# An LSTM step on one core: the cell update as a scan, with its gates' activations and a register load in other places

## The chip, the core and the metric

The program runs on one core of one Trainium2 chip, in a single launch. The metric is the device time of one execution in microseconds; several executions are summarised by their median. A core has engines that run side by side, each with its own in-order stream of instructions: TensorE (PE, with its weight loads shown as PEld), VectorE (DVE), ScalarE (ACT), GpSimd (POOL) and SyncE (SP, which issues DMAs). They meet through semaphores. An engine's sequencer reads its instructions and does the control work itself (register loads, branches, semaphore instructions); in the profile its records have the engine's name with a q behind it.

## The reference

Eight stages follow one another on a matrix x of 625 nodes by 512 features: four graph stages and four feed-forward ones. The change lies in the sixth, an LSTM over the 625 rows with four sets of weights. At each step the state chooses the set:

```python
def _lstm_activate(gates, c):
    i, f, g, o = jnp.split(gates, 4, axis=-1)
    c_new = jax.nn.sigmoid(f) * c + jax.nn.sigmoid(i) * jnp.tanh(g)
    h_new = jax.nn.sigmoid(o) * jnp.tanh(c_new)
    return (h_new, c_new)
...
def step(carry, x_t):
    h, c = carry
    sel_in = jnp.concatenate([h, c, x_t], axis=-1)
    logits = sel_in @ W_sel.T + b_sel
    onehot = jax.nn.one_hot(jnp.argmax(logits, axis=-1), Sx, dtype=x_t.dtype)
    g_all = jnp.einsum('bi,sgi->bsg', x_t, W_ih) + jnp.einsum('bh,sgh->bsg', h, W_hh) + b_ih + b_hh
    g = jnp.einsum('bsg,bs->bg', g_all, onehot)
    h2, c2 = _lstm_activate(g, c)
    return ((h2, c2), h2)
...
x = x + _L2_ffn_ref(_layernorm(x, axis=-1)[None], L2_ffn_W_ih, L2_ffn_W_hh, L2_ffn_b_ih, L2_ffn_b_hh, L2_ffn_W_sel, L2_ffn_b_sel)[0]
```

The batch is 1, H is 512, so each step is a product of one vector of 512 with a 512 by 2048 matrix, chosen by an argmax over four logits, and then some arithmetic on 512 numbers.

## The kernel before

`L2_ffn` prepares the stage. It multiplies all inputs with the input weights ahead of time into `gx`, splits the recurrent weights of the gates i, f and g into three bfloat16 parts (`wp`, L1591 to L1600) and keeps those of o in float32 (`wo`). The order of gates is i, f, g, o (`g` = 0, 1, 2, 3 in the code). Weights and inputs of g (`g == 2`) are multiplied by 2 at L1596, L1770 and L1772. It also computes, for each row and each of the four sets, a base for guessing the next step's set (`xv`, L1696 to L1733) from what the input alone says of the gates.

`recurrence` (L1820) is written by hand, outside the scheduler: one program for each engine, with semaphores set and waited for by name (`sem["c"]`, `sem["th"]` and so on). A vector of 512 lies as 128 partitions by 4 columns. The 625 steps run as 125 blocks of 5; inputs of a block are fetched by SyncE three blocks deep. One step goes like this:

- VectorE makes the new hidden state hT as `th` times `so` (L2092) and splits it into three bfloat16 parts (L2094, L2096).
- TensorE computes the logits in `lg`: the part of the cell state first (L1972, which waits for `c`), then the input row (L1974), then the part of hT (L1977). It doesn't wait for their argmax: it branches by a guess, made one step earlier, to the code of one of the four sets, runs a quarter of the output gate's matmuls (L2013) and 40 of the 48 matmuls of i and f into `pa` (L2016). Only then does it load the true choice into a register (L2018). If the guess was right, it goes on in the body `rest`; if not, it branches to `missed` and does those matmuls again with the right set.
- In `rest` follow the last 8 matmuls into `pa`, 48 for g into `pb` (twelve times four, L2025 to L2026), the output gate's other three quarters into `po` (L2028, L2030, both through L1993), one float32 matmul of a product needed much later (L2032, into `later`), and then the load of the next guess into a register (L2033, L2034) and the branch to the next step.
- VectorE meanwhile finds the argmax of the logits (`ix`) and the next guess (`gi`, L2107), turns `pa` (L2115), sums its parts into the first eight columns of `ga` (L2117: i and f), does the same with `pb` (L2119, L2121: g), and turns `po` (L2123).
- ScalarE takes tanh of half of all 12 columns of `ga` in one instruction (L2062, into `act4`), since sigmoid(v) is half of 1 + tanh(v/2). VectorE makes `prod` (L2126), which holds (1 + tanh(i/2)) tanh(g) and (1 + tanh(f/2)) times the kept state, and from it the new state (L2131), which is kept doubled as `c2`. Between the two it adds up the output gate (`go`, L2129). ScalarE takes sigmoid of `go` (L2064, `so`), then tanh of half of `c2` (L2066, `th`), and the step closes.

GpSimd does nothing in the loop but clear semaphores, in two ranges, `late` (after the logits) and `early` (after the first part of `ga`, L1958 to L1960, which then raises `ce`). VectorE waits for `ce` at L2124.

## Time and profile before

| what | value |
|---|---|
| time, median of 3 runs | 4764.43 us (4754.03 to 4769.32) |
| profiled execution | 4754.91 us, span 4753.1 us |
| mean granted TensorE clock | 0.965 |
| first and last L2092 in the recurrence's loop | 1519.9 and 4392.3 us |
| TensorE busy in the span | 4370.0 us (92%) |
| VectorE busy in the span | 2715.8 us (57%) |
| ScalarE busy in the span | 1231.4 us (26%) |

The profile is of one execution; its span runs from the first to the last instruction. Section 2 of its page cuts this span into 40 slices of 119 us, where a digit is a busy share in tenths:

```profile
PE   8998997799998999999999999999999999999888
...
DVE  7535015521264666666666666666666666666258
ACT  8533111211163222222222222222111111111136
```

The even stretch from the 13th slice to the 37th is the recurrence. Section 5 lists the costliest groups of instructions (line, engine, operation, tiles and shapes, count; then busy time, mean ns of one; then the engine's idle time before them and what ended it):

```profile
L1984 PE MATMUL pa<-wp,left 128*23 128x256 bf16 x32080 | 1003.3, 273 | 0.0
...
L1984 PE MATMUL pb<-wp,left 128*23 128x128 bf16 x30000 | 531.5, 219 | 0.0
...
L2064 ACT ACTIVATE so<-go 128x4 f32<-128x4 f32 x625 | 128.2, 205 | 282.5 <-DVE go L2129 282.5
```

Matmuls are pipelined: each of `pb`'s takes 219 ns, but they overlap. 30000 is 625 times 48.

### The profile page before, as it was taken

The numbers are of one execution on the slowest core, as the hardware profiler recorded it, in microseconds if no ns is written. First come the engines' busy times: TensorE is split into PE (matmuls) and PEld (weight loads), VectorE is DVE, ScalarE is ACT, GpSimd is POOL, SyncE is SP. The second block draws the span as 40 slices with busy tenths as digits, with TensorE's granted clock in tenths as the row PEclk, the third lists the DMA queues.
The fourth block names the chain that finished last, engine by engine and source line by source line (L and its number), as shares of the span: only waits on it lengthen the run. The fifth ranks groups of instructions, "written<-read, shape, count | busy, mean of one in ns | idle before, by whom it ended". The sixth has DMA issues, their size and how long they took to land. (4 is left out here: it accounts for less than half of the span.)

```text
span 4753.1 us, 246181 instructions
## 1 busy us (share of the span) xinstructions
PE 4370.0 (92%) x103068; PEld 3316.7 (70%) x103068; DVE 2715.8 (57%) x14167; ACT 1231.4 (26%) x4816; POOL 148.5 (3%) x152
## 2 busy tenths in 40 slices
PE   8998997799998999999999999999999999999888
PEld 6666764466566777777777777777777777777555
DVE  7535015521264666666666666666666666666258
ACT  8533111211163222222222222222111111111136
POOL 0000002300000000000000000000000000000011
PEclk9997997899999999999999999999999999999888
DMA  1131973611165122222222222221000000000200
GB/s 42 42 137 57 325 247 118 226 59 56 56 223 161 39 45 42 44 46 42 46 43 45 45 44 46 45 42 34 7 8 7 7 7 9 7 7 4 83 14 12
DMA packets 484662, 305.37 MB, mean 64 GB/s; under 512 B 287068, under 2 KB 385752, under 8 KB 483822
## 3 DMA queue, kind: packets, MB, share of 16 engines
q1 hardware_dynamic: 466554, 279.16, 21.6%
q0 software_dynamic: 8800, 16.92, 1.3%
q10 hardware_dynamic: 9092, 6.87, 0.6%
q8 instruction: 81, 1.33, 0.1%
q14 instruction: 135, 1.10, 0.1%
HBM read 256.29 MB, written 46.54 MB: 64 GB/s over the span
## 5 line engine op out<-in xcount | busy, mean ns | idle before, releaser
L1984 PE MATMUL pa<-wp,left 128*23 128x256 bf16 x32080 | 1003.3, 273 | 0.0
L1984 PEld LDWEIGHTS pa<-wp,left 128*23 128x23 bf16 x32080 | 800.1, 93 | 86.8 <-issue 0.3
L1993 PE MATMUL po<-w,left 128*1 128x128 f32 x15080 | 590.3, 273 | 4.9 <-issue 4.0
L1984 PE MATMUL pb<-wp,left 128*23 128x128 bf16 x30000 | 531.5, 219 | 0.0
L2062 ACT ACTIVATE act<-ga 128x12 f32<-128x12 f32 x625 | 132.7, 212 | 1481.2 <-DVE ga L2121 1481.2
L1984 PEld LDWEIGHTS pb<-wp,left 128*23 128x23 bf16 x30000 | 484.0, 94 | 4.6
L2115 DVE STREAM_TRANSPOSE col<-pa 128x256 f32<-128x256 f32 x625 | 281.7, 451 | 331.7 <-PE pa L1984 331.2
L1972 PE MATMUL pb<-wsel,act 128*4 128x8 f32 x5000 | 217.5, 170 | 178.3 <-DVE act L2131 162.1
L1972 PEld LDWEIGHTS pb<-wsel,act 128*4 128x4 f32 x5000 | 150.1, 83 | 329.3 <-DVE act L2131 312.4
L1993 PEld LDWEIGHTS po<-w,left 128*1 128x1 f32 x15080 | 314.9, 83 | 32.7 <-issue 15.6
L2032 PE MATMUL acc<-xslot,wslot 128*128 128x160 f32 x1250 | 336.9, 351 | 0.0
L2032 PEld LDWEIGHTS acc<-xslot,wslot 128*128 128x128 f32 x1250 | 185.8, 188 | 140.2 <-issue 140.2
L2057 ACT COPY xrow<-xlb 1x4 f32<-1x4 f32 x625 | 122.4, 196 | 538.4 <-ACTq L2055 538.4
L2123 DVE STREAM_TRANSPOSE col<-po 128x128 f32<-128x128 f32 x625 | 198.3, 317 | 92.9 <-PE po L1993 34.3
L2111 DVE COPY col<-gxb 128x16 f32 x625 | 114.1, 183 | 215.5 <-issue 215.5
L1977 PE MATMUL pb<-wsel,left 128*4 128x8 f32 x5000 | 217.5, 170 | 4.0 <-DVE left L2092 2.4
L1993 PE MATMUL po<-wo,left 128*1 128x128 f32 x5336 | 209.6, 272 | 4.7 <-issue 4.7
L2092 DVE TENSOR_TENSOR left<-th,so 128x4 f32<-128x4 f32 x625 | 104.3, 167 | 188.8 <-ACT th L2066 188.7
L2064 ACT ACTIVATE so<-go 128x4 f32<-128x4 f32 x625 | 128.2, 205 | 282.5 <-DVE go L2129 282.5
L2119 DVE STREAM_TRANSPOSE col<-pb 128x128 f32<-128x128 f32 x625 | 191.8, 307 | 1.0 <-PE pb L1984 1.0
L1977 PEld LDWEIGHTS pb<-wsel,left 128*4 128x4 f32 x5000 | 150.1, 83 | 60.1 <-DVE left L2092 6.0
L562 PE MATMUL wide<-hot_dst,hot_src 125*125 125x512 bf16 x640 | 178.0, 391 | 12.6 <-DVE hot_dst L542 12.6
(551 smaller groups left out, 6577.0 us busy)
## 6 DMA issues: line engine op xcount, KB each, us to landing
ring<-in_L_ffn_W_dram SPq DMA_DIRECT2D x80, 1024.0 KB
xslot<-xTd SPq DMA_DIRECT2D x384, 80.0 KB
wslot<-in_L_ffn_WihT_dram SPq DMA_DIRECT2D x384, 64.0 KB
gxb<-gx SPq DMA_DIRECT2D x124, 160.0 KB
w<-in_L_ffn_WihT_dram SPq DMA_DIRECT2D x16, 1024.0 KB
raw<-in_L_ffn_WhhT_dram SPq DMA_DIRECT2D x24, 512.0 KB
made<-ys SPq DMA_DIRECT2D x39, 256.0 KB
w<-in_L_gnn_Wl_dram SPq DMA_DIRECT2D x8, 1024.0 KB
```

Source lines behind the costliest of these rows:

```text
L562: nc.tensor.matmul(wide[i], hs[:, k], hd[:, :W0], start=first, stop=last)
L1972: pe.matmul(lg, c2[:, s:s + 1].to_broadcast([128, S]), wsel[:, 1, s], start=s == 0, stop=False)
L1977: m = pe.matmul(lg, hT[:, s:s + 1].to_broadcast([128, S]), wsel[:, 0, s], start=False, stop=s == KC - 1)
L1984: m = pe.matmul(out[32 * j:32 * j + 2 * GAP + 1], upper[:, s], wp[e][:, s, i, j, gs[0]:gs[1]].rearrange("p g n -> p (g n)"), start=k == 0, ...
L1993: m = pe.matmul(po[32 * j:32 * j + 1].rearrange("p (u r) -> p u r", r=32), left[:, s, 0:1], wo[e][:, s].rearrange("p (u j r) -> p j u r", ...
L2032: pe.matmul(later, wslot, xslot, start=False, stop=True, skip_group_check=True).then_inc(used)
L2057: act.copy(xrow[:, :S], xlb[b % DEEP][:, :, u + 1]).then_inc(sem["x"])
L2062: act.activation(act4[:, 0:3].rearrange("p g s -> p (g s)"), ga, AF.Tanh, scale=0.5).then_inc(sem["ifg"])
L2064: act.activation(so, go, AF.Sigmoid).then_inc(sem["so"])
L2115: dve.transpose(col[:, :8, :32], pa.rearrange("p (b r) -> p b r", r=32)).then_inc(sem["ta"])
L2119: dve.transpose(col[:, 8:12, :32], pb.rearrange("p (b r) -> p b r", r=32)).then_inc(sem["tb"])
L2123: dve.transpose(col[:, 12:, :32], po.rearrange("p (s r) -> p s r", r=32)).then_inc(sem["to"])
```

## The change

The state is kept as it is and not doubled, so the halving of the selection weights for it (L1630) goes. The tiles are new: `seq` is three rows of eight columns, `cs` eight columns whose odd ones (`cell_c`) are the state.

ScalarE now takes sigmoid of i and f (`ga[:, :8]`) as soon as the first part of `ga` is there, into the odd columns of two rows of `seq`, and raises the new semaphore `if`. tanh of g, into the even columns of the third row, follows when the second part is there. Then come tanh of the state and after it sigmoid of the output gate, in the opposite order to before. The new call for g has no scale, and the doubling at L1596, L1770 and L1772 stays.

VectorE multiplies sigmoid of f with the old state into the odd columns of the third row of `seq`, ahead of turning `po`. The wait for `ce` comes ahead of that turn too. One `tensor_tensor_scan` over eight columns then makes the new state: it walks along the columns with a running value, which it multiplies with a column of the first row and to which it adds a column of the third. The even columns of the first row are zero, so an even column gives tanh(g), and the odd one behind it sigmoid(i) tanh(g) + sigmoid(f) c. The sum for the output gate comes after the scan. hT now waits for `th` and for `so`.

TensorE loads the next guess amid the matmuls of g, after the sixth of their twelve groups of four, and no longer at the end of `rest`.

```diff
-            nc.vector.tensor_scalar_mul(wsel[:, 1], wsel[:, 1], 0.5)
...
-    act4, so = t_([128, 4, 4], "act4"), t_([128, 4], "so")
-    c2 = act4[:, 3]
-    prod = t_([128, 2, 4], "prod")
+    seq, cs, so = t_([128, 3, 8], "seq"), t_([128, 8], "cs"), t_([128, 4], "so")
+    cell_c = cs[:, 1::2]
...
-    nc.vector.memset(act4, 0.0)
+    nc.vector.memset(seq, 0.0)
...
-    late = "g x a ta b tb ga ifg o to ao pr c so th".split()
+    late = "g x a ta b tb ga if ifg o to ao pr c so th".split()
...
-                        pe.matmul(lg, c2[:, s:s + 1].to_broadcast([128, S]), wsel[:, 1, s], start=s == 0, stop=False)
+                        pe.matmul(lg, cs[:, 2 * s + 1:2 * s + 2].to_broadcast([128, S]), wsel[:, 1, s], start=s == 0, stop=False)
...
                         for k in range(12):
                             ms = list(gates(e, pb, (2, 3), k))
+                            if k == 5:
+                                pe.wait_ge(sem["g"], 1)
+                                pe.reg_load(guess, gi[e:e + 1, 0:1])
                         ms[-1].then_inc(sem["b"])
...
-                        pe.wait_ge(sem["g"], 1)
-                        pe.reg_load(guess, gi[e:e + 1, 0:1])
                         pe.br(name("next"))
...
+                    act.wait_ge(sem["ga"], 1)
+                    act.activation(seq[:, 0:2, 1::2], ga[:, :8].rearrange("p (g s) -> p g s", g=2), AF.Sigmoid).then_inc(sem["if"])
                     act.wait_ge(sem["ga"], 2)
-                    act.activation(act4[:, 0:3].rearrange("p g s -> p (g s)"), ga, AF.Tanh, scale=0.5).then_inc(sem["ifg"])
+                    act.activation(seq[:, 2, 0::2], ga[:, 8:], AF.Tanh).then_inc(sem["ifg"])
+                    act.wait_ge(sem["c"], 1)
+                    act.activation(th, cell_c, AF.Tanh).then_inc(sem["th"])
                     act.wait_ge(sem["ao"], 1)
                     act.activation(so, go, AF.Sigmoid).then_inc(sem["so"])
-                    act.wait_ge(sem["c"], 1)
-                    act.activation(th, c2, AF.Tanh, scale=0.5).then_inc(sem["th"])
...
                         wait("th")
+                        wait("so")
                         dve.tensor_tensor(hT, th, so, ALU.mult).then_inc(sem["h"])
...
+                        wait("if")
+                        dve.tensor_tensor(seq[:, 2, 1::2], seq[:, 1, 1::2], cell_c, ALU.mult).then_inc(sem["pr"])
+                        wait("ce").then_inc(sem["ce"], -1)
                         wait("o")
                         dve.transpose(col[:, 12:, :32], po.rearrange("p (s r) -> p s r", r=32)).then_inc(sem["to"])
-                        wait("ce").then_inc(sem["ce"], -1)
+                        wait("pr")
                         wait("ifg")
-                        dve.scalar_tensor_tensor(prod, act4[:, 0:2], 1.0, act4[:, 2:4], op0=ALU.add, op1=ALU.mult
-                                                 ).then_inc(sem["pr"])
+                        dve.tensor_tensor_scan(cs, seq[:, 0], seq[:, 2], 0.0, op0=ALU.mult, op1=ALU.add).then_inc(sem["c"])
                         wait("to")
                         dve.tensor_tensor(go, col[:, 12:, 0], col[:, 12:, 3 * GAP], ALU.add).then_inc(sem["ao"])
-                        wait("pr")
-                        dve.scalar_tensor_tensor(c2, prod[:, 1], 0.5, prod[:, 0], op0=ALU.mult, op1=ALU.add
-                                                 ).then_inc(sem["c"])
```

More of the change, by code (lines that the diff above doesn't have):

```diff
@@ L2060, in _ @@
                         m.then_inc(free[b % DEEP][1])
+                    act.wait_ge(sem["ga"], 1)
+                    act.activation(seq[:, 0:2, 1::2], ga[:, :8].rearrange("p (g s) -> p g s", g=2), AF.Sigmoid).then_inc(sem["if"])
                     act.wait_ge(sem["ga"], 2)
-                    act.activation(act4[:, 0:3].rearrange("p g s -> p (g s)"), ga, AF.Tanh, scale=0.5).then_inc(sem["ifg"])
+                    act.activation(seq[:, 2, 0::2], ga[:, 8:], AF.Tanh, scale=0.5).then_inc(sem["ifg"])
+                    act.wait_ge(sem["c"], 1)
+                    act.activation(th, cell_c, AF.Tanh).then_inc(sem["th"])
                     act.wait_ge(sem["ao"], 1)
                     act.activation(so, go, AF.Sigmoid).then_inc(sem["so"])
-                    act.wait_ge(sem["c"], 1)
-                    act.activation(th, c2, AF.Tanh, scale=0.5).then_inc(sem["th"])
                     if n < len(LATER) and n % 4 == 3:
@@ L2082, in _ @@
                 dve.tensor_copy(xrow[:, :S], xlb[0][:, :, 0]).then_inc(sem["x"])
-                dve.memset(c2, 0.0).then_inc(sem["c"])
+                dve.memset(cs, 0.0).then_inc(sem["c"])
+                dve.memset(th, 0.0).then_inc(sem["th"])
+                wait("th")
                 dve.memset(so, 0.0).then_inc(sem["so"])
-                wait("so")
-                dve.memset(th, 0.0).then_inc(sem["th"])
                 for b in range(BLOCKS):
@@ L2135, in _ @@
                 wait("th")
+                wait("so")
                 dve.tensor_tensor(hist[:, N], th, so, ALU.mult)
```

## The prediction

> **What bounds the kernel now.** I read the page's busy row first, then busy time in three stretches, then who waited for whom, then one step of the recurrence in order of time, and last the records of TensorE's own queue (its sequencer), which the order of time leaves out.

> The recurrence runs from 1519.9 to 4396.6 us: 2876.7 of the span's 4753.1 us, in 625 steps that each begin with L2092. The 624 distances between them average 4.603 us. TensorE is busy in 2692 of those 2877 us, but the steps are serial: what counts is the chain inside one step. This one, from the middle, took 4.45 us from hT to hT (2401.76 to 2406.21); its second half:

> ```profile
> 2403.75 0.85 PE L1984 MATMUL pb<-wp,left 128*23 128x128 bf16 x48
> 2404.06 0.45 DVE L2115 STREAM_TRANSPOSE col<-pa 128x256 f32<-128x256 f32 x1 [0.41 <-PE pa L1984]
> 2404.37 0.60 PEld L1993 LDWEIGHTS po<-w,left 128*1 128x1 f32 x24
> 2404.42 0.84 PE L1993 MATMUL po<-w,left 128*1 128x128 f32 x24
> 2404.54 0.20 DVE L2117 TENSOR_REDUCE ga<-col 128x8 f32<-128x32 f32 x1
> 2404.66 0.30 DVE L2119 STREAM_TRANSPOSE col<-pb 128x128 f32<-128x128 f32 x1
> 2405.00 0.18 DVE L2121 TENSOR_REDUCE ga<-col 128x4 f32<-128x16 f32 x1
> ...
> 2405.21 0.21 ACT L2062 ACTIVATE act<-ga 128x12 f32<-128x12 f32 x1 [2.24 <-DVE ga L2121]
> 2405.33 0.32 DVE L2123 STREAM_TRANSPOSE col<-po 128x128 f32<-128x128 f32 x1 [0.15 <-PE po L1993]
> 2405.57 0.12 DVE L2126 SCALAR_TENSOR_TENSOR prod<-act 128x8 f32<-128x8 f32 x1
> 2405.68 0.17 DVE L2129 TENSOR_TENSOR go<-col 128x4 f32<-128x4 f32 x1
> ...
> 2405.76 0.16 DVE L2131 SCALAR_TENSOR_TENSOR act<-prod 128x4 f32<-128x4 f32 x1
> 2405.88 0.20 ACT L2064 ACTIVATE so<-go 128x4 f32<-128x4 f32 x1 [0.46 <-DVE go L2129]
> ...
> 2405.99 0.19 ACT L2066 ACTIVATE th<-act 128x4 f32<-128x4 f32 x1
> ...
> 2406.21 0.17 DVE L2092 TENSOR_TENSOR left<-th,so 128x4 f32<-128x4 f32 x1 [0.29 <-ACT th L2066]
> ```

> Columns: start, duration, engine, line, operation, and the idle time before it with what ended it. The tail to see: TensorE's output-gate matmuls end at 2405.26, VectorE turns them at 2405.33, and only after this (back to back, 0.24 us later) come prod, go and c2; ScalarE then does sigmoid of go, and tanh of c2 behind it. hT waits for that tanh, L2066. An engine's answer starts some 0.03 us after the result it waits for.

> ```profile
> ACT act L2062 <- DVE ga L2121: 1481.2, 625, 4.3
> ...
> DVE left L2092 <- ACT th L2066: 188.7, 624, 0.8
> ```

> This, from the waits (total, times, longest), shows that hT waits for th in every step, and that ScalarE idles over 2 us per step before L2062: room for another activation.

> ```profile
> L2018 PEldq TENSOR_LOAD <-ix x677: 298/302/417, 1522.2 to 4393.3; - x170
> L2034 PEldq TENSOR_LOAD <-gi x625: 298/302/315, 1525.4 to 4395.0; - x157
> ```

> A register load holds TensorE's sequencer for 0.302 us. L2018 ran 677 times in 625 steps: 52 guesses missed, each with the 40 matmuls again. Steps with a hit have a median of 4.447 us, missed ones 6.105: a miss costs 1.658.

> **The change, part by part**, on the step above, +/- where another step differs.

> Scan for prod and c2. f times c (128x4; by go's row 0.165) needs sigmoid of f only. ga's first eight columns are ready at 2404.74, so that sigmoid runs 2404.77 to 2404.98 (L2062's 0.21) in ScalarE's idle time; f times c goes behind L2121 at about 2405.10, in VectorE's 0.15 idle before L2123. Cost nothing; without that cover it would cost the 0.085 to 0.12 that separates such instructions' starts. tanh of g stays where L2062 was. The scan takes prod's place at 2405.57. The trace of before has no scan: nearest rows are prod's 0.124 (same 128x8) and the 0.203 of L2117 (128x32). I take 0.165, the usual small VectorE operation. The state is ready at 2405.735 instead of 2405.92.

> Tanh before sigmoid. th runs from 2405.77; go keeps its place (it needs the transpose's end, 2405.65, ends 2405.85); so starts at 2405.88, where it did before, and ends at 2406.08. hT starts 0.03 later, at 2406.11 to 2406.12: 0.09 sooner. The output gate takes over as the last wait, so the other 0.09 of the state's lead buys nothing. By the scan's lower end still 0.09; by its upper, th holds so back and 0.06 is left. hT's second wait costs nothing while th comes over 0.1 us before so; where L2115 has two waits, 0.073 lies between the record of the first and the start.

> POOL's ce is now waited for before L2123. POOL's clear (L1959) ends 0.23 us before the time f times c is due; not late. The lost scaling at L1630 is one small operation outside the loop: nothing. At the ends of the 125 blocks the loop's own moves end some 0.1 us before hT now; I allow 0 to 6 us.

> The moved register load. Before, it was read while 20 slow matmul passes of L1993 lay queued, and nothing waited. Now it comes behind 24 of pb's 48 matmuls; behind it, on TensorE's queue, are the other 24, the 12 output-gate matmuls and the later one. Waiting for g is free (gi was ready at 2403.13), but while the load runs nothing new enters the queue. What is needed: 0.302 plus, by L2021, 0.056 from the sequencer's resuming to the first matmul of an empty queue, plus 0 to 0.063 (the distance from L2034's end to the sequencer's next record): 0.36 to 0.42. What covers it: matmuls already queued, each 14 ns in pb (0.056 for four). At L2018 the sequencer is 24 matmuls ahead, with pa's 27 ns each; at L2029, in pb itself, 16 ahead, about 0.03 before the next four begin, and after L2021 it needs nearly 0.4 us to issue these 32 anyway. 24 ahead cover 0.34 to 0.36, 16 ahead 0.25. So TensorE stalls 0 to 0.06 by the one, 0.11 to 0.17 by the other. I take 0.14, by L2029, whose place is 24 matmuls away in the same run. It delays po in full, and go, so, hT with it; L2119 too, since pb's end now comes just in time for it. The end of the step gains nothing from the load's absence: the branches behind it are done before the state is ready.

> [...]

> The state itself. Weights and input part of g are doubled at L1596, L1770 and L1772, and the old tanh halved them; the new call has no scale, so the state takes tanh of 2g, while guesses are still built from tanh of g (L1703). The kernel's flow then differs in how often it misses. Nothing in the trace says how often: from no change (52) to twice as many (104), 0 to 86 us. The guess also holds 0.45 of the true logits and the known input part, so I take a third more, 17 misses: 28 us.

> **The sum.** Per step -0.09 + 0.14 = +0.05; by 624 steps +31; misses +28: +59. The profiled execution took 4754.9 (span 4753.1): 4814. That execution lies 9.5 below the median of the three runs, whose own spread is 15.

> **Rivals.** (1) The load is covered: 24 matmuls or more are queued, the stall is 0 to 0.06. Then -0.09 to -0.03 per step, about -37 us, and with the misses unchanged 4718 (4699 at no stall). For it: L2018's 24 and no stall there; against: L2029's 16. It decides from a cover of 0.27 to 0.33 us up. (2) Misses double: +86 in place of +28, 4872. For it: every step's g is another; against: the guess's larger parts are not. (3) The scan or the swapped activations are slower than the rows: at 0.26 the scan gives the whole 0.09 back, +56, 4870; against: none of VectorE's operations of this size reaches 0.21 outside transposes. (4) The change doesn't do what it says: if sigmoid of i and f waited for both parts of ga, ScalarE would have it behind tanh of g, and f times c would come after L2123: some 0.1 more, 4876; the separate wait for ga at 1 speaks against it.

> **How the numbers follow.** Load exposed, misses up moderately: 0.62. (1) 0.22, (2) 0.09, (3) 0.04, (4) 0.03. A tenth is left out below 4712 and above 4880 each (4880: stall 0.17, 45 misses more). Within the likeliest case alone: 4775 to 4860. 0.3% is 14 us, about what this kernel's runs can tell. Faster by more needs (1) with few new misses: 0.20; the same: (1) with some misses, or a stall near 0.08: 0.12; slower: 0.68.

> **What would show it.** Right: a gap of over 0.1 us between pb's sixth and seventh group of matmuls; L2123 starting later after L2115 than the 1.27 here; so, not th, ending hT's wait; so starting as soon as go ends; the load of ix counted some 694 times. Wrong: pb's 48 matmuls still in 0.85 us; a scan over 0.2; loads of ix near 677 or far above 700; a wait of L2123 on POOL.

## The result and the profile after

The changed kernel takes 4775.09 us (median of 7 runs, 4770.24 to 4781.35); the kernel before, run in the same comparison, 4763.77 us (7 runs, 4752.51 to 4769.32). The ratio is 1.003, with a 95% interval of 1.0017 to 1.0044: slower by some 11 us. The forecast was 59 us more than the profiled execution of before.

First a correction, since a number of the forecast hangs on it. The diff above and the words around it give the new call for tanh of g without a scale. The call in the changed kernel (its L2063) has one:

```diff
+                    act.activation(seq[:, 2, 0::2], ga[:, 8:], AF.Tanh, scale=0.5).then_inc(sem["ifg"])
```

So the doubling of g at L1596, L1770 and L1772 is halved again, as before, and the state is the same quantity in both kernels. The sentence "the new call for g has no scale" is a misreading of mine, and so is everything that the forecast built on it.

In the tables below a step is counted from 0 and goes from one start of hT (L2092 before, L2094 now) to the next. The span grew from 4753.1 to 4775.3 us, by 22.2. Of this, 7.8 lie ahead of the recurrence, whose first hT moved from 1519.9 to 1527.7; in the traces of the experiments below, which share that part with the changed kernel, that start lies anywhere from 1521 to 1533, so a shift of this size says nothing of the change. The 624 steps went from 2872.3 to 2887.1 us, +14.8, and what follows them from 360.9 to 360.5. What is to be explained is the +14.8: mean step 4.603 before, 4.627 now. A hit step is one with a single load of ix, that is, a right guess. The first five steps, 30 to 39 us together in each trace, are left out of every median of hit steps and of every count of long ones below; the sums over 624 steps hold them.

The page of the changed kernel, its first lines and three of its groups (line, engine, operation, tiles, count; busy time and mean ns of one; idle time before and what ended it):

```profile
span 4775.3 us, 248057 instructions
...
PE 4388.7 (92%) x103068; PEld 3331.1 (70%) x103068; DVE 2720.9 (57%) x14166; ACT 1389.1 (29%) x5441; POOL 148.6 (3%) x152
...
L1982 PE MATMUL pa<-wp,left 128*23 128x256 bf16 x32080 | 1003.2, 273 | 0.7 <-PEq L2019 0.6
...
L1982 PE MATMUL pb<-wp,left 128*23 128x128 bf16 x30000 | 536.1, 219 | 0.1
...
L2094 DVE TENSOR_TENSOR left<-th,so 128x4 f32<-128x4 f32 x625 | 104.6, 167 | 245.0 <-ACT so L2067 244.8
```

Two of the forecast's reasons fall here. `pa` has 32080 matmuls, as many as before: no step more misses its guess. `pb` has no idle time in front of its matmuls, though the register load now lies in the middle of them. The last line names what holds hT now: so, with 244.8 us of waiting, where before it was th with 188.7.

One hit step in order of time (step 182, 4.425 us long; columns as in the view of before):

```profile
2386.56 0.85 PE L1982 MATMUL pb<-wp,left 128*23 128x128 bf16 x48
2386.86 0.45 DVE L2117 STREAM_TRANSPOSE col<-pa 128x256 f32<-128x256 f32 x1 [0.41 <-PE pa L1982]
...
2387.23 0.84 PE L1991 MATMUL po<-w,left 128*1 128x128 f32 x24
...
2387.58 0.21 ACT L2061 ACTIVATE seq<-ga 128x8 f32<-128x8 f32 x1 [1.80 <-DVE ga L2119]
2387.81 0.18 DVE L2123 TENSOR_REDUCE ga<-col 128x4 f32<-128x16 f32 x1
2387.90 0.15 DVE L2125 TENSOR_TENSOR seq<-seq,cs 128x4 f32<-128x4 f32 x1
...
2388.14 0.32 DVE L2128 STREAM_TRANSPOSE col<-po 128x128 f32<-128x128 f32 x1
2388.38 0.14 DVE L2131 TENSOR_TENSOR_SCAN cs<-seq 128x8 f32<-128x8 f32 x1
2388.49 0.17 DVE L2133 TENSOR_TENSOR go<-col 128x4 f32<-128x4 f32 x1
2388.55 0.20 ACT L2065 ACTIVATE th<-cs 128x4 f32<-128x4 f32 x1 [0.32 <-DVE cs L2131]
...
2388.69 0.20 ACT L2067 ACTIVATE so<-go 128x4 f32<-128x4 f32 x1
...
2388.99 0.17 DVE L2094 TENSOR_TENSOR left<-th,so 128x4 f32<-128x4 f32 x1 [0.34 <-ACT so L2067]
```

The tail is the one that was forecast: sigmoid of i and f lies in ScalarE's idle time, f times c fits between L2123 and the turn of `po`, the scan takes 0.14, th runs early and so ends last. The turn of `po` starts 1.28 after L2117; before it was 1.27. What was not forecast stands in the last two lines: so ends at 2388.69 + 0.20 = 2388.89, and hT starts at 2388.99, 0.10 later. Before, hT started 0.03 after th.

The records of the queues show where these 0.10 come from (count; shortest, median and longest ns; first and last start). Here is the kernel before, VectorE's own semaphore instructions:

```profile
L2079 DVEq EVENT_SEMAPHORE  x1875: 21/21/21, 1521.7 to 4395.8; - x188
```

and the same line of the changed kernel:

```profile
L2080 DVEq EVENT_SEMAPHORE  x3126: 21/21/21, 1527.7 to 4419.2; - x196
```

3 of them per step have become 5 (1875 and 3125 in 625 steps; the one left over stands behind the loop). So one wait rides on the instruction itself, and where the code writes two ahead of it, the other becomes an instruction of its own. The change made two such places, the scan (`pr`, `ifg`) and hT (`th`, `so`). At hT the semaphore instruction starts at 2388.927, right after so ends, and hT itself 0.066 after that: it is the wait written last that stands alone, and here it is the late one.

A second thing shows when the steps are laid side by side by their number modulo 20 (four blocks of five). The ordinary hit step fell from 4.447 to 4.425. But the last step of every fourth block (number 4 of 20) takes 4.813, and the four after it 4.573, 4.558, 4.534 and 4.556. The end of such a step, number 184, in order of time:

```profile
2397.54 0.20 ACT L2067 ACTIVATE so<-go 128x4 f32<-128x4 f32 x1
...
2398.25 0.17 DVE L2094 TENSOR_TENSOR left<-th,so 128x4 f32<-128x4 f32 x1 [0.74 <-ACT so L2067]
```

so ends at 2397.74, hT starts at 2398.25: 0.51 later and not 0.10. VectorE's queue has its semaphore instruction at 2397.80, behind the moves that close a block's loop, and then nothing for 0.43 us until hT. No semaphore that hT waits for, no DMA packet and no engine's result falls in this gap; SyncE issues a DMA in it, as it does around the hT that ends step 182, which came 0.10 after so. These steps cost (4.813 - 4.425) x 31 + 0.13 x 124 = 28 us, an estimate from the medians; by the means, the hit steps lie 0.0395 above their median over 567 steps, 22 us, where before they lay 3 us below it.

### The profile page after: what moved, and what is told of

The parts are those of the page before. It is cut to its first block, busy times and chain, and to the rows that moved or that the text cites. A ratio compares the mean times of both kernels' runs of the same rounds, so it can differ in the third digit from the quotient of the medians.

```text
span 4775.3 us, 248057 instructions
## 1 busy us (share of the span) xinstructions
PE 4388.7 (92%) x103068; PEld 3331.1 (70%) x103068; DVE 2720.9 (57%) x14166; ACT 1389.1 (29%) x5441; POOL 148.6 (3%) x152
## 5 line engine op out<-in xcount | busy, mean ns | idle before, releaser
L2061 ACT ACTIVATE seq<-ga 128x8 f32<-128x8 f32 x625 | 131.3, 210 | 1200.2 <-DVE ga L2119 1200.2
L2117 DVE STREAM_TRANSPOSE col<-pa 128x256 f32<-128x256 f32 x625 | 281.5, 450 | 331.0 <-PE pa L1982 331.0
L1970 PEld LDWEIGHTS pb<-wsel,cs 128*4 128x4 f32 x5000 | 150.2, 83 | 186.2 <-DVE cs L2131 167.3
L1970 PE MATMUL pb<-wsel,cs 128*4 128x8 f32 x5000 | 217.5, 170 | 35.2 <-issue 9.5
L2094 DVE TENSOR_TENSOR left<-th,so 128x4 f32<-128x4 f32 x625 | 104.6, 167 | 245.0 <-ACT so L2067 244.8
L2121 DVE STREAM_TRANSPOSE col<-pb 128x128 f32<-128x128 f32 x625 | 196.2, 314 | 1.6 <-PE pb L1982 0.5
L2065 ACT ACTIVATE th<-cs 128x4 f32<-128x4 f32 x625 | 128.2, 205 | 197.4 <-DVE cs L2131 197.4
```

What stands on the lines that cost most here:

```text
L1970: pe.matmul(lg, cs[:, 2 * s + 1:2 * s + 2].to_broadcast([128, S]), wsel[:, 1, s], start=s == 0, stop=False)
L2061: act.activation(seq[:, 0:2, 1::2], ga[:, :8].rearrange("p (g s) -> p g s", g=2), AF.Sigmoid).then_inc(sem["if"])
L2065: act.activation(th, cell_c, AF.Tanh).then_inc(sem["th"])
L2117: dve.transpose(col[:, :8, :32], pa.rearrange("p (b r) -> p b r", r=32)).then_inc(sem["ta"])
L2121: dve.transpose(col[:, 8:12, :32], pb.rearrange("p (b r) -> p b r", r=32)).then_inc(sem["tb"])
```

## The experiments

Two causes were put up: the order of the two waits at hT, and a late place in VectorE's code that the loop meets in every fourth block. Against them stood the forecast's own (the moved load stalls TensorE) and the swapped activations (th ahead of so). The line numbers of an experiment can differ by a few from those of the changed kernel.

**Waits at hT in the other order.**

```diff
-                        wait("th")
                         wait("so")
+                        wait("th")
                         dve.tensor_tensor(hT, th, so, ALU.mult).then_inc(sem["h"])
```

> The changed kernel with the two waits ahead of hT in the other order: first so, then th. Theory W (the second wait costs): in the changed kernel's trace the wait that is written last becomes a semaphore instruction of its own on VectorE's sequencer; so comes last and is that one, and hT starts 0.105 us after so's end where 0.033 was usual. With th in that place hT should start 0.03 to 0.04 after so: 0.07 less in some 470 to 620 steps, 33 to 43 us, about 4735 to 4742. Theory P (my prediction: two waits cost nothing while th is early): no change, 4775.

Measured: 4753.24 us, 0.9977 of before (0.9968 to 0.9985). An ordinary step's end, in order of time:

```profile
2379.84 0.20 ACT L2065 ACTIVATE th<-cs 128x4 f32<-128x4 f32 x1 [0.32 <-DVE cs L2131]
...
2379.98 0.20 ACT L2067 ACTIVATE so<-go 128x4 f32<-128x4 f32 x1
...
2380.22 0.17 DVE L2094 TENSOR_TENSOR left<-th,so 128x4 f32<-128x4 f32 x1 [0.27 <-ACT so L2067]
```

hT comes 0.033 after so (median over the steps; 0.103 in the changed kernel), and the ordinary step is 4.356, by 0.091 shorter than before. The 624 steps fell by 21.8 us. The time fell by less than expected (4735 to 4742), because the slow steps stayed as they were (4.812, 4.575) and a block's last step did not gain at all (4.443): there the loop's own moves, which in the changed kernel end 0.006 after so (median of numbers 9, 14 and 19 of 20; 0.086 before it where no block ends), hold hT.

**VectorE's code moved, nothing else.** Some tiny memsets of a tile that nothing reads, once, ahead of the loop over the blocks; 20 of them, and 41.

```diff
+    blank = t_([128, 20], "blank")
...
+                for _ in range(20):
+                    dve.memset(blank[:, _:_ + 1], 0.0)
                 for b in range(BLOCKS):
```

> The changed kernel with 20 small memsets of an unused tile on VectorE ahead of the loop, which do nothing but move the loop's code by 20 instructions. Theory C (code place): every fourth block of five steps has the boundary of a piece of VectorE's code between the wait for so and hT; that costs 0.38 us in 31 steps and some 0.12 in 124 others, 27 us. With the boundary in a place where VectorE waits for TensorE anyway, 15 to 27 us go: 4748 to 4760, and steps 4 to 8 of each 20 look like the others. Rival: those steps are slow for another reason (ScalarE's code, DMAs), then nothing changes but the memsets' 2 us.

> The same with 41 memsets: the boundary then comes about nine instructions ahead of where it is, near the scan, where VectorE works on the path. Theory C: still slow steps in one block of four, but with the late instruction elsewhere (near the scan or the transpose of po); 4760 to 4780. Rival (any shift helps, or none does): as with 20 memsets.

Measured: with 20, 4749.76 us, 0.9972 (0.9961 to 0.9982); with 41, 4753.26 us, 0.9984 (0.9973 to 0.9994). With 20 no hit step beyond the first five is over 4.6 us, and the 624 steps took 23.6 us less than in the changed kernel, though there is more work in it. Step 184, which took 4.834, now ends so:

```profile
2385.14 0.20 ACT L2068 ACTIVATE so<-go 128x4 f32<-128x4 f32 x1
...
2385.47 0.17 DVE L2097 TENSOR_TENSOR left<-th,so 128x4 f32<-128x4 f32 x1 [0.36 <-ACT so L2068]
```

0.13 from so to hT in place of 0.51; the step is 4.447. The late place has moved on to VectorE's register load of ix, which starts 0.32 late in one step of 20, at a point where VectorE would wait for `pa` anyway. With 41, I expected the slow steps to be there still (4760 to 4780), and this missed. The late place did move to where I expected it, the semaphore instruction ahead of the scan; but the turn of `po` still runs there and covers most of it: in one step of 20 the scan starts only 0.04 late. So the place decides, but how far the code must be moved for it to come back isn't shown by this pair.

**One VectorE instruction more in each block** (a memset ahead of the inner loop), so that the block's code has another length.

```diff
                     there(dve, b)
+                    dve.memset(blank[:, b:b + 1], 0.0)
                     gxs = gxb[b % DEEP].rearrange("p (e g) u c -> p e g u c", e=S)
```

> The changed kernel with one more instruction in the code of each block, a memset of an unused column ahead of the five steps' loop. Theory C, made exact: VectorE's code comes in pieces of which the changed kernel's blocks are exactly a quarter, so the boundary falls at the same place in every fourth block; with one instruction more it wanders, as it does in the kernel before. Then no steps of over 4.6 us at a distance of 20; a few here and there; 10 to 20 us less than the changed kernel, 4755 to 4765, for all the added memsets. Rival: the distance of 20 steps is given by something else (ScalarE's code, the fetches of three blocks): still 31 slow steps at a distance of 20.

Measured: 4757.85 us, 0.9996 (0.9984 to 1.0007). The hit steps over 4.6 us fell from 35 to 18, and they no longer come back after 20 steps (number 4 of 20 has a median of 4.461, numbers 5 to 8 together of 4.425). The 624 steps took 17.2 us less with 125 instructions more: it is not the amount of code but where its lengths put it.

**Both: waits in the other order, and 20 memsets.**

> Both mendings at once: the wait for so written ahead of that for th, and the 20 memsets ahead of the loop. If the two costs are separate they add: the swap alone took 22 us off the recurrence, and left its steps 4 to 8 of each 20 as slow as before (the code boundary holds hT there, not so); with the boundary away these 155 steps should gain the 0.07 too, 10 us more. 22 + 24 + 10 = some 55 us less than the changed kernel, 4720 to 4728, and ordinary steps of 4.356. Rival: one cause behind both, then no better than 4748.

Measured: 4727.37 us, 0.9929 (0.9916 to 0.9941), the fastest of all kernels here, 35 us below the kernel before in the same comparison (4762.77). The median lengths of hit steps by their number modulo 20, and the 624 steps together, in us:

| steps | before | changed | waits | 20 memsets | both |
|---|---|---|---|---|---|
| 13 (an ordinary one) | 4.443 | 4.424 | 4.355 | 4.425 | 4.356 |
| 4 (block's last) | 4.447 | 4.813 | 4.812 | 4.444 | 4.445 |
| 6 | 4.447 | 4.558 | 4.558 | 4.422 | 4.357 |
| 14 (block's last) | 4.448 | 4.443 | 4.443 | 4.443 | 4.443 |
| 624 steps | 2872.3 | 2887.1 | 2865.3 | 2863.5 | 2839.5 |

The two causes add: the waits give 21.8 alone and 24.0 on top of the memsets, the memsets 23.6 alone and 25.8 on top of the waits. Without the first five steps, which differ from trace to trace, they add to the tenth: the waits 21.0 alone and 20.9 on top, the memsets 24.9 and 24.8. The whole balance of the recurrence is then 2839.5 - 2872.3 = -32.8 for the edit itself, and +47.6 for the two: +14.8.

**Then also the two waits at L2117.** There `gs` is written ahead of `a`, which comes late: the same form. The two were exchanged in the kernel with both changes.

```diff
-                        wait("gs")
                         wait("a")
+                        wait("gs")
                         dve.transpose(col[:, :8, :32], pa.rearrange("p (b r) -> p b r", r=32)).then_inc(sem["ta"])
```

> As f1, and the waits ahead of the turn of pa in the other order too (a first, then gs), so that a, which comes last, is no semaphore instruction of its own. The turn should start 0.04 to 0.07 sooner. Theory: no gain, since the turn of pb, two instructions later, waits for pb's end, which comes just then, and the turn of po for po: within 5 us of f1. Rival: everything behind it moves up, 0.07 in 620 steps, 43 us less.

Measured: 4728.37 us, 0.9931 (0.9918 to 0.9944), and 2839.9 in the recurrence: no difference. The turn of `pa` does start 0.071 sooner (2.216 us after hT and not 2.287, medians of the hit steps), but the turn of `pb`, two instructions on, starts at 2.888 and not 2.892, since it waits for the end of `pb`'s matmuls. Here a late wait written last cost time only where no slack lay behind it: 0.070 at hT, nothing at the turn of `pa`.

**The register load back at the end of `rest`**, the rest of the change kept.

```diff
                             ms = list(gates(e, pb, (2, 3), k))
-                            if k == 5:
-                                pe.wait_ge(sem["g"], 1)
-                                pe.reg_load(guess, gi[e:e + 1, 0:1])
...
                         pe.matmul(later, wslot, xslot, start=False, stop=True, skip_group_check=True).then_inc(used)
+                        pe.wait_ge(sem["g"], 1)
+                        pe.reg_load(guess, gi[e:e + 1, 0:1])
```

> The changed kernel with the load of the guess back at the end of the body. Theory W/C (the load amid g is covered by queued matmuls): no change, 4775 within 5. Theory P (my prediction, the load stalls TensorE 0.14 per step): 87 us less. A third possibility: the end of the step needs the load gone (the branches would come late for the earlier state): some us more.

Measured: 4772.79 us, 1.0022 (1.0012 to 1.0032); 2885.4 in the recurrence, 1.7 less. Its group of `pb` on the page:

```profile
L1982 PE MATMUL pb<-wp,left 128*23 128x128 bf16 x30000 | 531.4, 219 | 0.0
```

With the load amid them these matmuls were busy 4.7 us longer over 625 steps, 0.007 per step: this is all that the trace shows of the stall that was put at 0.14.

**The load doubled.** A second load of the same register behind the first.

```diff
                                 pe.reg_load(guess, gi[e:e + 1, 0:1])
+                                pe.reg_load(guess, gi[e:e + 1, 0:1])
```

> The changed kernel with the load of the guess done twice amid g's matmuls (the second loads the same value). It measures the cover: the sequencer was 24 matmuls ahead there, some 0.34 to 0.36 us of pb's pace, and one load of 0.30 showed no stall. A second load of 0.30 to 0.36 should have almost no cover left: 0.28 to 0.40 us per step, 175 to 250 us, 4950 to 5025. By my prediction's reckoning (16 ahead) the first would have stalled already. Rival: loads are hidden in another way (their results are fetched while the queue goes on being filled): under 30 us.

Measured: 4777.38 us, 1.0029 (1.0018 to 1.004). This says nothing of the load: TensorE's queue shows only one per step.

```profile
L2028 PEldq TENSOR_LOAD <-gi x625: 296/300/510, 1537.3 to 4421.8; - x157
```

The first, whose value the second would overwrite, is not in the code that ran. It is a repeat of the changed kernel.

**The load at other places**, in its stead: behind the first of `pb`'s twelve groups, and at the head of `rest`, ahead of the last eight `pa` matmuls, where TensorE's queue is empty.

```diff
-                            if k == 5:
+                            if k == 0:
                                 pe.wait_ge(sem["g"], 1)
```

> The load behind the first of the twelve groups of pb's matmuls and not the sixth. From the sequencer's return it has sent 12 matmuls by then; at 9.5 to 12 ns each the load starts near 1.78 after hT, ends near 2.08, and the next matmul could begin near 2.14, where it is due at 2.045. Theory: 0.06 to 0.12 us per step, 35 to 75 us, 4810 to 4850, with the gap behind the first group of pb. Rival as before: 4775.

> The changed kernel with the load of the guess at the head of the body behind a hit, ahead of the last 8 matmuls into pa. There the sequencer has just come back from the other load, the branch and a wait, and only some 4 matmuls are queued, 0.11 us at pa's pace. Theory (a load costs what the queue doesn't cover): 0.302 + 0.056 - 0.11, about 0.2 to 0.27 us per step, 125 to 170 us, 4900 to 4945. Rival (a register load doesn't hold the queue up): 4775.

Measured: behind the first group 4833.49 us, 1.0146 (1.0129 to 1.0163); at the head 4988.13 us, 1.0475 (1.0457 to 1.0492). In the first of the two, step 182 has

```profile
2400.34 0.94 PE L1982 MATMUL pb<-wp,left 128*23 128x128 bf16 x48
```

where the changed kernel has 0.85: the gap behind the first group is 0.134 in place of 0.055, a stall of 0.079. The hit step's median is 4.505, by 0.080 longer. In the second, between `pa`'s tenth and eleventh group:

```profile
2442.43 0.14 PEld L1982 LDWEIGHTS pa<-wp,left 128*23 128x23 bf16 x8 [0.41 <-issue]
2442.46 0.40 PE L1982 MATMUL pa<-wp,left 128*23 128x256 bf16 x8 [0.15 <-issue]
2442.57 0.78 PEld L1982 LDWEIGHTS pb<-wp,left 128*23 128x23 bf16 x48
2442.68 0.85 PE L1982 MATMUL pb<-wp,left 128*23 128x128 bf16 x48
```

TensorE's weight loads stand idle for 0.41 with nothing but their own queue to wait for; the groups start 0.441 apart instead of 0.109, and the step has 4.758, by 0.333 more. This is above the 4900 to 4945 that were expected, since the load also begins 0.10 after the queue's record ahead of it. So a load does stall TensorE, and by what the matmuls already queued do not cover: 0.33 with none queued, 0.08 behind the first group of `pb`, 0.007 at most behind the sixth. The records of all 567 hit steps give the number to this. From the start of the load to the first matmul behind it pass 0.359, 0.358 and 0.359 us (medians; at the head, behind the first group, behind the sixth), with 0, 8 to 12 and 24 of `pa`'s and `pb`'s matmuls waiting in the queue when the load begins. The 24 last just as long: 24 x 0.014 = 0.34, from a first one that begins 0.02 after the load.

**so ahead of th again**, on ScalarE.

```diff
+                    act.wait_ge(sem["ao"], 1)
+                    act.activation(so, go, AF.Sigmoid).then_inc(sem["so"])
                     act.wait_ge(sem["c"], 1)
                     act.activation(th, cell_c, AF.Tanh).then_inc(sem["th"])
-                    act.wait_ge(sem["ao"], 1)
-                    act.activation(so, go, AF.Sigmoid).then_inc(sem["so"])
```

> The changed kernel with sigmoid of the output gate ahead of tanh of the state on ScalarE again. By the trace tanh starts 0.14 us ahead of sigmoid now; in the other order it would have to wait for go and then run behind sigmoid: th ends some 0.10 later than so does now, and hT with it, with th now the wait that is no instruction of its own: 0.105 - 0.033 = 0.07 come back. So +0.03 in most steps, 10 to 25 us more than the changed kernel, 4785 to 4800. If the order didn't matter: 4775. If it is worth the whole 0.10: 4835.

Measured: 4784.8 us, 1.0049 (1.0033 to 1.0064); 2897.7 in the recurrence, 10.6 more than the changed kernel. hT then starts 0.033 after th, whose wait is written first, and the hit step's median is 4.450. With th ahead the tail ends 0.09 sooner, and with the waits as they stand 0.07 of this are lost again.

## Why the prediction was wrong, point by point

- **"I take 0.14"** (stall of the moved load, +87 us of the sum): failed. It measured 0.00 to 0.01, and putting the load back gave 1.7 us. The forecast had two readings of how far TensorE's queue runs ahead, 24 matmuls by L2018 and 16 by L2029, and chose the second because its place was nearer. In the trace the load starts at 2386.536, with the first of `pb` just beginning (2386.56): all 24 matmuls ahead of it were queued, in this step as in all 567. What the load needs, put at 0.36 to 0.42, measured 0.359; the cover was the term that was mis-sized. That is rival (1), whose cover of 0.34 to 0.36 held; its time of 4718 (4699 at no stall) did not, for the two reasons below.
- **"17 misses: 28 us"**: failed, by the misread line. 677 loads of ix, 52 misses, as before. A diff's line on which a term hangs has to be read in the whole kernel too.
- **"The scan takes prod's place ... I take 0.165"**: right in kind, 0.133 measured, near the lower row. **"Tanh before sigmoid ... 0.09 sooner"**: right. Median over the steps, so ends 4.320 after hT, where th ended at 4.414: 0.094. With the waits exchanged the whole of it arrives: 4.356 in place of 4.447.
- **"hT's second wait costs nothing while th comes over 0.1 us before so"**: failed, and it is the largest step that the runs showed in place of the load. th did come 0.14 before so. But it is the wait written last that becomes a separate instruction, and so's was the last. The same sentence named the price, 0.073 by L2115; it was left out of the sum. Measured: 0.070 per ordinary step, and 22 to 24 us in all, since block ends and the steps with a late place gain little or nothing.
- **"At the ends of the 125 blocks ... 0 to 6 us"**: too small. With the two causes undone, a block's last step takes 4.445 and the ordinary one 4.356: 0.089 x 125 = 11 us of the expected gain do not come.
- **Sigmoid of i and f apart, f times c, ce ahead of the turn, POOL**: costed at nothing, and right; no wait for POOL shows in VectorE's waits.
- **Not in the forecast at all**: the late place in VectorE's code, 24 to 26 us.

The edit as forecast without stall and misses would be 624 x -0.09 = -56. With both causes undone the recurrence shows -32.8. Of the rest, 11 are the block ends, and about 11 the first four steps of every fourth block (4.438 to 4.458 in the kernel with both, some 0.09 x 124), where the late place still takes part: the loop's move behind its branch comes 0.08 to 0.10 late there.

The signs of the wrong terms hid them: a stall and misses that never were (+115) stood in for a wait and a code place that were (+47.6), so the forecast called the slower side for reasons that do not hold.

## What to carry to other kernels

When an instruction waits for two things, write the wait that comes last first in the code, and read from the engine's own queue which one stands alone: here 22 to 24 us hung on two lines. A register load in TensorE's queue cost in these runs what the matmuls queued ahead of it did not cover (0.36 us, less the cover), so place it where the trace shows the queue furthest ahead, and not where its value is needed. When a loop in the changed kernel is slow in every n-th pass only, with a gap that no semaphore explains, move the code by a few instructions before judging the edit.

## What the runs showed of the hardware

The trace has transfers that fit. One line of the changed kernel's page, in its list of DMA queues (packets, MB, share):

```profile
q14 instruction: 142, 1.16, 0.1%
```

In the recurrence lie 83 of these packets, each of 8192 bytes. The queue's records don't say for which engine a packet is, but after the late hT of every fourth block one of them starts, in all 31 cases, 0.51 to 1.26 us after that hT starts. With 20 memsets they come in all 31 cases in the step whose load of ix is late, 2.1 to 2.8 us after its hT: they move with the late place, though only VectorE's code was changed. So transfers of this queue are shown to go with the gap. That the gap is a wait for code isn't: these packets start behind it, and what fills the 0.43 us in which nothing shows stays open. The 128 instructions are no more than the estimate above; no record gives them.
